# A graph layer on one core: the attention's projection in half-size products, another place for the MLP's token sums, two key loads on another queue, and an earlier start of the graph's steps

## The chip, the cores and the metric

The kernel runs on one core of a Trainium2 chip. Its time is device microseconds (us) of one execution; the number compared is the median of several executions. The engines have short names: PE is TensorE (matrix products, with PEld for its weight loads), DVE is VectorE, ACT is ScalarE, POOL is GpSimd, SP is SyncE. SP, ACT and POOL also issue transfers (DMA). Each engine works through its own queue in order, so an instruction that waits holds up all that stand behind it on that engine.

## What is computed

All data is 32-bit float. 1250 nodes with 768 features go through three blocks, whose results are added to the features:

```python
xn = layernorm(x)                                   # [1250, 768]
x1 = x + gnn(xn) + mix(xn)
out = x1 + ffn(layernorm(x1))

def gnn(xn):            # two layers of graph attention, 4 heads of 192, then 2 heads of 96
    e = leaky_relu(s_src[src] + s_dst[dst], 0.2)    # 21250 edges with the loops
    ee = exp(e - segment_max(e, dst)[dst])
    out = segment_sum(ee / segment_sum(ee, dst)[dst] * h[src], dst)
    ...

def mix(x):
    q, k, v = split(layernorm(x) @ qkv_w + qkv_b)   # 12 heads of 64
    q, k = elu(q) + 1, elu(k) + 1
    kv = einsum('sd,se->de', k, v)                  # per head
    y = (q @ kv) / (q @ k.sum(0))
    x = x + y @ proj_w + proj_b                     # the projection
    h = gelu(layernorm(x) @ fc1_w + fc1_b) @ fc2_w + fc2_b   # the MLP, 768 -> 3072 -> 768
    return x + h

def ffn(x):             # 4 experts of 768 -> 1536 -> 768; the router picks 2 for all nodes
    ...
```

## The kernel before

The tokens lie in 10 tiles of 125. Tokens 0 to 624 and 625 to 1249 are treated as two halves, since most large products are made by Strassen's scheme (Winograd's form): both operands are cut into quarters, four sums are made on each side, and seven half-size products take the place of eight. `combined` (and `seven_weights`) makes the four sums of the weights' side, `differences` (and `by_tokens`) the four of the tokens' side; one of each four overwrites a quarter in place. `product` issues a half product as three accumulating matmuls. Each 32-bit matmul instruction shows as two records in the trace.

The order of the work:

1. Weights are folded, x is normalized, x @ Wu is made (L545). Meanwhile the graph's edges are turned into a dense table of edge counts: in 10 pieces of 17 columns of 125 edges each, DVE compares the edges' keys (loaded as rows, `kr`, by `load_keys` and `later_pieces`) with the piece's own keys, and POOL writes each column by an indirect transfer that adds into one of two tables in memory (`tab`, L315; 170 in all, columns alternate between the tables). The tables are cleared by SP's transfers of `pattern`. The keys of pieces 0 to 3 are loaded by POOL's queue (L276), pieces 4 to 9 by SP's.
2. The graph's first features (L578), then keys and values, then queries of the attention (`keys_pair`, `values_pair`, `queries`). `divided` makes the attention's denominators (a small product `ps_z`, a reciprocal L943, a product L944), `project` folds kv into the projection's weights `pm`.
3. The projection: for each tile and each half of the output columns six accumulating matmuls (L974), added by DVE (L979) to the normalized features, which come back from memory (`xn_d`). After each group of tiles (`order2`) come moments (L409), a normalization (L997), transposes (L1004) and scalings by `affine` (odd blocks on ACT, even ones on DVE, L372). When the last tile is through, the tokens' side of the MLP, `xt`, gets memory that the attention's tiles have left, and `by_tokens` fills it (L105).
4. The MLP in 12 groups of 256 hidden columns, each with two units of tokens (250 and 375 of either half): `fc1_unit` yields after each of its seven half products, `fc2_half` makes two matmuls for one tile and one half of the output columns (L1077) and DVE adds them (L1082). A string, `PPhhhhPhhPPhhPPhhhh` and the like, sets how products (P) and halves (h) alternate.
5. The graph attention is a generator, `gnn()`, whose steps are spread over the MLP: after every P and h `spend` adds to a credit, and each step taken costs some. The credit starts at -44, so that the first step comes 42 us of nominal work after spending begins, and spending begins with the first group's second unit. The graph's first step merges the two tables (`merged`, L1115), fetches the rows of the sum (L1128), and DVE turns each fetched block of 125 rows into `far` (L1143), from which running maxima per head are made (L1151, L1147). The products of the attention weights follow (L1255, L1294).
6. The expert layer (L81, L1655) and the output.

The framework assigns memory by pools that open and close, adds the semaphores, and fixes each engine's order when the kernel is built; `pin` keeps an instruction in the order of the program.

Of the kernel before, what the change touches and what calls it, by code (L numbers as in the profile page):

```python
# [8 lines left out]
F32 = mybir.dt.float32  # L9
# [23 lines left out]
def tile_gps_layer(ctx, tc, a, out):  # L33
# [6 lines left out]
    def bcast(ap, p):  # L40
        return ap.partition_broadcast(p)
# [181 lines left out]
    arow = ep.tile([TP, 2, D], F32, name="arow")  # L223
    nc.sync.dma_start(arow[:, 0, :], bcast(a["L0_gnn_bu"], TP))
    nc.sync.dma_start(arow[:, 1, :], bcast(a["L0_mix_fc2_b"], TP))
    kvb = rp.tile([128, 2, D], F32, name="kvb")
    kb, vb = kvb[:TP, 0, :], kvb[:, 1, :]
    nc.sync.dma_start(kb, bcast(a["L0_mix_qkv_b"][D : 2 * D], TP))
    nc.sync.dma_start(vb, bcast(a["L0_mix_qkv_b"][2 * D : 3 * D], 128))
    ones = ep.tile([96, TP], F32, name="ones")  # L230
    nc.gpsimd.memset(ones, 1.0)

# [8 lines left out]
        )  # L241
        pin(nc.gpsimd.dma_start(key_d, key))

    kcol = rp.tile([TP, EC], F32, name="kcol")

    def columns():
        ps = bank4("ps_key")
# [10 lines left out]
    )  # L258


    counts_of = rp.tile([128, TP], BF16, name="counts_of")
# [307 lines left out]
    for t in range(NT):  # L569
# [40 lines left out]
            nc.sync.dma_start(brow_d, arow[0:1, 0, :])  # L610
        if t == 8:
            edges.close()
            mk = mix.enter_context(tc.tile_pool(name="mk", bufs=1, side="right"))

            def between(name):
                return mk.tile([128, 384], F32, name=name, bufs=2)
# [17 lines left out]
    with tc.tile_pool(name="kvp", bufs=1) as kvp:  # L634
# [13 lines left out]
        kvbd = mk.tile([128, KC, 128], F32, name="kvbd")  # L648
        ksum = mk.tile([128, KC, 128], F32, name="ksum")
# [245 lines left out]
    with tc.tile_pool(name="qp", bufs=1) as qp:  # L895
# [56 lines left out]
                if 4 <= n < 10:  # L952
                    project(n - 4)
        acc, xn = xn, acc
        divided(5, (0,))
        rest_of = [1, 2, 3]


        mv2 = const.tile([TP, NT, 2], F32, name="mv2")
        r2 = const.tile([TP, NT, 2], F32, name="r2")  # L960
        order2 = [(0, 1, 5, 6), (2, 3, 7), (4, 8), (9,)]
        for part in order2:
            for t in part:
                by_parts(nc.sync, xn[:, t, :], xn_d[t])
        at = 0
        for part in order2:
            where = {t: at + i for i, t in enumerate(part)}
            ts = slice(at, at + len(part))
            at += len(part)
            for t in part:  # L970
                for c0, w in HALVES:
                    ps = bank("ps_p")
                    for k in range(KC):
                        nc.tensor.matmul(  # L974
                            ps[:TP, :w], qT[:, k, t * TP : (t + 1) * TP], pm[:, k, c0 : c0 + w],
                            start=k == 0, stop=k == KC - 1,
                        )
                    o = xn[:, t, c0 : c0 + w]
                    nc.vector.tensor_tensor(o, ps[:TP, :w], o, ALU.add)  # L979
                    if rest_of:  # L980
                        divided(5, (rest_of.pop(0),))
# [12 lines left out]
            for t in part:  # L994
                z = qp.tile([TP, D], F32, name="z2", bufs=2)
                i = where[t]
                nc.scalar.activation(  # L997
                    z, xn[:, t, :], AF.Identity, bias=r2[:, i, 1:2], scale=r2[:, i, 0:1]
                )
                for j in range(2):  # L1000
                    ps = bank4("ps_t")
                    for i in range(3):
                        k = 3 * j + i
                        nc.tensor.transpose(  # L1004
                            ps[:, i, :TP], z[:, k * 128 : (k + 1) * 128], ident[:TP, :TP]
                        )
                    for i in range(3):
                        k = 3 * j + i
                        affine(
                            fT[:, k, t * TP : (t + 1) * TP], ps[:, i, :TP], k, "ln2_w", "ln2_b"  # L1010
                        )
# [382 lines left out]
    for g in range(GROUPS):  # L1394
        if g:
            load_fc1(g + 1)
            load_fc2(g, 1)
            load_fc2(g + 1, 0)
        for c, pattern in enumerate(("PPhhhhPhhPPhhPPhhhh", "PPhhPhhPPhhPPhh")):
            if g == GROUPS - 1 and c:  # L1400
                for _ in steps:
                    pass
                cost = None
                gnn_pool.__exit__(None, None, None)
            parts = fc1_unit(g, c)
            for p in pattern:
                if p == "P":
                    next(parts)
                    if g or c:
                        spend(2.04 if c else 1.36)  # L1410
                elif todo:
                    put_half(*todo.pop(0))
            todo = halves_of(g, c)
    for x in todo:
        put_half(*x)
    turned(ready[0])

    t9 = NT - 1
# [442 lines left out]
```

## Time and profile before

| what | value |
|---|---|
| median of 3 runs (lowest, highest) | 1904.69 us (1903.83, 1906.24) |
| the profiled execution: its time, its span | 1900.13 us, 1898.2 us |
| busy: PE, PEld, DVE, ACT, POOL | 1869.0, 1245.7, 1336.0, 803.3, 498.0 us |
| mean granted TensorE clock | 0.994 |
| the table's scatters on POOL (L315) | 57.2 to 562.3 us, 170 |
| the projection (L974) | 432.9 to 520.6 us, 240 records |
| first matmul of the MLP, last of its halves | 521.2 us, 1330 us |
| the graph's first instruction on DVE (L1143) | 590.5 us |

Times in the profile are us from the span's start. In a line of the timeline the columns are start, length, engine, source line, operation, what is written and read, shapes, number of instructions, and in brackets how long the engine had been idle and what ended that. A wait view tells "who <- for whom: us in total, times, longest". The span is 1.93 us shorter than the execution.

### The profile page before, as it was taken

To read this page: it belongs to the slowest core of one execution; us is meant where nothing else is said; L and a number is where in the kernel's file an instruction comes from. 1 tells how busy PE (TensorE), PEld (TensorE's weight loads), DVE (VectorE), ACT (ScalarE), POOL (GpSimd) and SP (SyncE) were. 2 spreads that over 40 slices of the span, in tenths; PEclk is the share of its full clock that TensorE was granted. 3 is DMA by queue.
4 is the path that set the end of the run, shared out by engine and by line. 5 is a ranking of instruction groups with operands and counts; after the bars stand their busy time and mean duration, and the time that the engine had idled before them with its cause. 6 is when DMAs were issued, how large, how long until landed. Compare 5 with 4: busy or idle time off the path is not lost.

```text
span 1898.2 us, 19544 instructions
## 1 busy us (share of the span) xinstructions
PE 1869.0 (98%) x6966; PEld 1245.7 (66%) x6966; DVE 1336.0 (70%) x2407; ACT 803.3 (42%) x1207; POOL 498.0 (26%) x341
## 2 busy tenths in 40 slices
PE   9999999999998999999999999999999999999998
PEld 7555556865565668787777655566766666666664
DVE  4656692677546967676666977766677777777778
ACT  3233221331321128777674186645364353433330
POOL 2265766687882110111111121000221000000000
PEclk9999999999998999999999999999999999999999
DMA  9748532523139751233343532202485201011023
GB/s 341 238 97 213 114 85 52 134 19 49 2 30 187 136 145 55 70 95 88 106 113 79 151 111 73 69 9 67 126 101 82 71 0 67 3 64 47 12 87 109
DMA packets 184285, 175.50 MB, mean 92 GB/s; under 512 B 110043, under 2 KB 153595, under 8 KB 182908
## 3 DMA queue, kind: packets, MB, share of 16 engines
q0 software_dynamic: 126640, 68.01, 20.8%
q1 hardware_dynamic: 54270, 98.48, 16.4%
q10 hardware_dynamic: 3278, 7.75, 1.3%
q8 instruction: 55, 0.90, 0.2%
q14 instruction: 42, 0.34, 0.1%
HBM read 137.80 MB, written 42.05 MB: 95 GB/s over the span
## 4 chain that ended last, share of the span: by engine, by line
PE 91%; DMA 4%; POOL 1%; DVE 1%; issue 1%; ACT 1%; SPq 0%; DVEq 0%; POOLq 0%; ACTq 0%
PE ps_f L1077 14%; PE ps_p L81 13%; PE ps_r L81 12%; PE ps_o L1255 7%; PE ps_a L127 7%; PE ps_g L578 4%; PE ps_u L545 4%; PE ps_p L974 4%; PE ps_c L127 3%; PE ps_f L1655 3%; PE ps_o L1294 2%; PE ps_va L127 2%; PE ps_ka L127 2%; PE ps_qa L127 2%; PE ps_d L127 2%; POOL tab L315 1%
## 5 line engine op out<-in xcount | busy, mean ns | idle before, releaser
L315 POOL DMA_INDIRECT tab<-mult,place_e x170 | 351.1, 2065 | 157.7 <-DMA tab<-mult,place_e 102.6
L1077 PE MATMUL ps_f<-w,v 128*125 128x384 f32 x960 | 338.9, 487 | 6.9 <-DVE slot_a L1082 6.9
L1077 PEld LDWEIGHTS ps_f<-w,v 128*125 128x125 f32 x960 | 178.0, 188 | 113.4 <-DVE slot_a L1082 8.0
L1082 DVE TENSOR_TENSOR slot_a<-ps_f,slot_a 125x384 f32<-125x384 f32 x240 | 131.6, 553 | 66.6 <-PE ps_f L1077 62.7
L1210 DVE TENSOR_TENSOR wt<-ee 125x375 f32<-125x375 f32 (+1 forms) x180 | 105.9, 590 | 84.5 <-PE ps_o L1255 57.5
L1255 PEld LDWEIGHTS ps_o<-turns,wt 125*125 125x125 f32 x800 | 137.1, 188 | 29.1 <-DVE wt L1211 4.0
L1255 PE MATMUL ps_o<-turns,wt 125*125 125x193 f32 x800 | 151.7, 329 | 2.9 <-DVE wt L1211 2.9
L1205 ACT ACTIVATE ee<-bt,s 125x375 f32<-125x375 f32 (+1 forms) x180 | 114.8, 638 | 77.1 <-DVE wt L1210 69.8
L81 PE MATMUL ps_p<-fT,w 128*128 128x312 f32 (+1 forms) x432 | 125.5, 426 | 0.6 <-ACT c L1573 0.6
L1211 DVE SCALAR_TENSOR_TENSOR wt<-wt,slot_x 125x375 f32<-125x375 f32 (+1 forms) x180 | 105.9, 590 | 4.4
L81 PEld LDWEIGHTS ps_p<-fT,w 128*128 128x128 f32 x432 | 81.5, 189 | 36.2 <-ACT c L1573 1.1
L81 PE MATMUL ps_r<-w,slot_a 128*125 128x384 f32 x260 | 94.5, 486 | 0.0
L127 PE MATMUL ps_a<-fT,w 128*128 128x250 f32 (+1 forms) x288 | 86.8, 432 | 0.7 <-DVE slot_a L979 0.7
L1617 DVE SCALAR_TENSOR_TENSOR slot_x<-ps_r,gate,slot_x 125x384 f32<-125x384 f32 x100 | 60.7, 615 | 33.3 <-PE ps_r L81 33.0
L81 PE MATMUL ps_p<-xt,ws 128*128 128x313 f32 (+1 forms) x288 | 83.6, 426 | 0.0
L578 PE MATMUL ps_g<-fx,zT 128*125 128x388 f32 x240 | 80.2, 490 | 1.5 <-DVE zT L372 1.5
L545 PE MATMUL ps_u<-wu,fT 128*125 128x384 f32 x240 | 79.9, 487 | 0.4 <-ACT fT L531 0.4
L974 PE MATMUL ps_p<-wp,slot_x 128*125 128x384 f32 x240 | 79.9, 486 | 0.0
L1147 DVE SCALAR_TENSOR_TENSOR slot_x<-turns,s,slot_x 125x1250 f32<-125x1250 f32 x54 | 79.4, 1512 | 0.1
L1026 ACT ACTIVATE v<-v,par 128x250 f32<-128x250 f32 (+1 forms) x72 | 40.0, 556 | 88.0 <-DVE v L1046 41.3
L1208 ACT ACTIVATE ee<-bt,s1l 125x375 f32<-125x375 f32 (+1 forms) x120 | 75.4, 628 | 0.1
L81 PE MATMUL ps_r<-w2s,ht 128*125 128x384 f32 x200 | 72.7, 486 | 0.0
(403 smaller groups left out, 3413.0 us busy)
## 6 DMA issues: line engine op xcount, KB each, us to landing
turns<-g_d POOLq DMA_DIRECT2D x12, 942.4 KB, 14.2
w<-in_L_mix_fc_w_dram SPq DMA_DIRECT2D x12, 768.0 KB
w<-in_L_mix_fc_w_dram SPq DMA_DIRECT2D x24, 384.0 KB
slot_x<-tab POOLq DMA_DIRECT2D x14, 610.4 KB, 6.6
w<-in_L_ffn_w_dram SPq DMA_DIRECT2D x11, 768.0 KB
w<-in_L_ffn_w_dram SPq DMA_DIRECT2D x5, 1536.0 KB
slot_x<-tab POOLq DMA_DIRECT2D x40, 183.1 KB, 3.3
kr_l<-key_d SPq DMA_DIRECT2D x6, 1062.5 KB
```

The costliest lines, as they stand in the source:

```text
L81: return lambda *args, **kw: pin(getattr(self.engine, name)(*args, **kw))
L127: engine.matmul(ps, wt[:, k, :], x[:, k, :], start=k == 0 and not more, stop=k == n - 1, skip_group_check=more,)
L315: nc.gpsimd.indirect_dma_start(out=tabs[c % 2][:, :], out_offset=bass.IndirectOffsetOnAxis(ap=place[:, c : c + 1], axis=0), in_=mult[:, c ...
L545: nc.tensor.matmul(ps[:TP, :w], fT[:, k, tc_], wu[:, k, c0 : c0 + w], start=k == 0, stop=k == KC - 1,)
L578: nc.tensor.matmul(ps[:TP, :388], zT[:, k, :], fx[:, k, h2 * 388 : (h2 + 1) * 388], start=k == 0, stop=k == KC - 1,)
L974: nc.tensor.matmul(ps[:TP, :w], qT[:, k, t * TP : (t + 1) * TP], pm[:, k, c0 : c0 + w], start=k == 0, stop=k == KC - 1,)
L1077: nc.tensor.matmul(ps, v_of[c][:, f, h, at : at + TP], lasts[g, j][:, f, :], start=f == 0, stop=f == 1,)
L1082: nc.vector.tensor_tensor(o, ps, o, ALU.add)
L1205: nc.scalar.activation(e[:, 0, :w], bt[:TP, 0, :w], AF.Exp, bias=s[:, 0, h, c : c + 1])
L1210: nc.vector.tensor_tensor(wt[:, :w], e[:, 0, :w], e[:, 1, :w], ALU.max)
L1211: nc.vector.scalar_tensor_tensor(wt[:, :w], wt[:, :w], 1.0, adj, op0=ALU.min, op1=ALU.mult)
L1255: nc.tensor.matmul(sums[i // 2][:TP, (i % 2) * 193 : (i % 2 + 1) * 193], wt[:, i * TP : (i + 1) * TP], gh[:, c, :], start=c == 0 and i % 2 ...
```

## The change

The diff does six things. The projection is made by seven half products for each pair of tiles t and t + 5 (`projected`), with the weights' sums in `wsum` and the tokens' differences in the memory of the query weights (`xq`); `order2` becomes four parts of 2, 2, 4 and 2 tiles. A place `room` of 9 x 625 columns is opened when the edges' first memory closes; it holds the key and value biases (loaded there and then, no longer at the start), `kvbd`, `ksum` and the attention's intermediates (`between`), and later `xt`. `by_tokens` of the MLP's first unit and the first group's weight sums move from the end of the last part to the end of the third. In all but the last part all scalings go to ACT. The keys of pieces 2 and 3 are loaded by SP. The graph's credit starts at -20 instead of -44, its pace is 1.01 instead of 1.05, and the string of the first group's second unit changes.

```diff
-    rp = mix.enter_context(tc.tile_pool(name="rp", bufs=1, side="right"))
...
-    kvb = rp.tile([128, 2, D], F32, name="kvb")
-    kb, vb = kvb[:TP, 0, :], kvb[:, 1, :]
-    nc.sync.dma_start(kb, bcast(a["L0_mix_qkv_b"][D : 2 * D], TP))
-    nc.sync.dma_start(vb, bcast(a["L0_mix_qkv_b"][2 * D : 3 * D], 128))
...
-            load_keys(i + 2, nc.gpsimd)
+            load_keys(i + 2, nc.sync)
...
-    def affine(o, v, k, wname, bname):
-        if k % 2:
+    def affine(o, v, k, wname, bname, scalar=False):
+        if k % 2 or scalar:
...
         if t == 8:
             edges.close()
+            xt_pool = ExitStack()
+            xt_room = xt_pool.enter_context(tc.tile_pool(name="xt_room", bufs=1, side="right"))
+            room = xt_room.tile([128, 9 * HALF], F32, name="room")
+            kvb = room[:, : 2 * D].rearrange("p (j d) -> p j d", d=D)
+            kb, vb = kvb[:TP, 0, :], kvb[:, 1, :]
+            nc.sync.dma_start(kb, bcast(a["L0_mix_qkv_b"][D : 2 * D], TP))
+            nc.sync.dma_start(vb, bcast(a["L0_mix_qkv_b"][2 * D : 3 * D], 128))
+            kvbd, ksum = (
+                room[:, c : c + D].rearrange("p (k n) -> p k n", n=128) for c in (2 * D, 3 * D)
+            )
+            turn = {}
+            def between(name):
+                n = turn[name] = turn.get(name, -1) + 1
+                c = 4 * D + 384 * (2 * ("c1", "u2", "ex").index(name) + n % 2)
+                return room[:, c : c + 384]
...
-        divided(5, (0,))
-        rest_of = [1, 2, 3]
+        xq = wq_of[0].rearrange("p k d -> p (k d)")[:, : 4 * 9 * TP].rearrange(
+            "p (u a b n) -> p u a b n", u=4, a=3, b=3
+        )
+        def pair_differences(t):
+            of = (
+                qT[:, k : k + 3, h * HALF + t * TP : h * HALF + (t + 1) * TP]
+                for k in (0, 3) for h in (0, 1)
+            )
+            differences(nc.vector, of, xq[:, t % 4], 0, TP)
+        def projected(t):
+            cs, ds = slice(t * TP, (t + 1) * TP), slice(HALF + t * TP, HALF + (t + 1) * TP)
+            x11, x21, x22, t3 = qT[:, 0:3, cs], qT[:, 3:6, cs], qT[:, 3:6, ds], qT[:, 0:3, ds]
+            t1, t2, t4 = (xq[:, t % 4, i] for i in range(3))
+            pa, pd, pc = (bank(n)[:TP, :384] for n in ("ps_pa", "ps_pd", "ps_pc"))
+            w11, w12 = pm[:, 0:3, 0:384], pm[:, 3:6, 0:384]
+            def put(o, ps):
+                nc.vector.tensor_tensor(o, ps, o, ALU.add)
...
+            product(nc.tensor, pa, x11, w11)
+            put(y11, pa)
+            yield
+            product(nc.tensor, pd, x21, w12)
+            put(y11, pd)
+            yield
+            _, _, s3, w22, s1, s2, s4 = sevens["p"]
+            product(nc.tensor, pa, t2, s2, more=True)
+            put(y21, pa)
+            yield
+            product(nc.tensor, pc, t1, s1)
+            put(y22, pc)
+            yield
+            product(nc.tensor, pa, t3, s3, more=True)
+            put(y22, pa)
+            yield
+            product(nc.tensor, pc, x22, s4, more=True)
+            put(y21, pc)
+            yield
+            product(nc.tensor, pa, t4, w22, more=True)
+            put(y12, pa)
+            yield
...
-        order2 = [(0, 1, 5, 6), (2, 3, 7), (4, 8), (9,)]
+        order2 = [(0, 5), (1, 6), (2, 7, 3, 8), (9, 4)]
...
+        pairs2 = [projected(t) for t in range(NT // 2)]
+        take(pairs2[0], 2)
+        take(pairs2[1], 2)
+        sevens["p"] = seven_weights(pm, wsum)
+        pair_differences(0)
+        xt = room.rearrange("p (a b n) -> p a b n", a=3, b=3)
...
+            for t in part[::2]:
+                t = t % 5
+                if t:
+                    pair_differences(t)
+                for i, _ in enumerate(pairs2[t]):
+                    if t == 0 and i < 4:
+                        divided(5, (i,))
...
-            if at == NT:
-                mix.close()
-                mix_t = mlps.enter_context(tc.tile_pool(name="mix_t", bufs=1, side="right"))
-                xt = mix_t.tile([128, 3, 3, HALF], F32, name="xt")
-                by_tokens(nc.vector, xt, *MIX[0])
-                fc1_sums(0)
...
-            if at == NT:
-                by_tokens(nc.vector, xt, *MIX[1])
+            if part[0] == 2:
+                by_tokens(nc.vector, xt, *MIX[0])
+                fc1_sums(0)
+        mix.close()
+        by_tokens(nc.vector, xt, *MIX[1])
...
-    credit, cost = -44.0, 0.0
+    credit, cost = -20.0, 0.0
...
-        credit += 1.05 * us
+        credit += 1.01 * us
...
+            if g == 0 and c:
+                pattern = "PhPhhPhhhPhhPPP"
```

More of the change, by code (lines that the diff above doesn't have):

```diff
@@ L242, in compute_keys @@
         pin(nc.gpsimd.dma_start(key_d, key))
-    kcol = rp.tile([TP, EC], F32, name="kcol")
+    kcol = lw.tile([TP, EC], F32, name="kcol")
     def columns():
@@ L258, in tile_gps_layer @@
     )
-    counts_of = rp.tile([128, TP], BF16, name="counts_of")
+    counts_of = lw.tile([128, TP], BF16, name="counts_of")
     nc.gpsimd.memset(counts_of, 256.0)
@@ L612, in tile_gps_layer @@
             edges.close()
+            xt_pool = ExitStack()
[13 more added lines that the diff above has]
+                return room[:, c : c + 384]
             mk = mix.enter_context(tc.tile_pool(name="mk", bufs=1, side="right"))
-            def between(name):
-                return mk.tile([128, 384], F32, name=name, bufs=2)
             edges = ExitStack()
@@ L647, in tile_gps_layer @@
             pin(nc.vector.memset(same[b, b], 1.0))
-        kvbd = mk.tile([128, KC, 128], F32, name="kvbd")
-        ksum = mk.tile([128, KC, 128], F32, name="ksum")
         p_kv = [bank4("ps_kv"), bank4("ps_kv")]
@@ L954, in tile_gps_layer @@
         acc, xn = xn, acc
-        divided(5, (0,))
-        rest_of = [1, 2, 3]
+        xq = wq_of[0].rearrange("p k d -> p (k d)")[:, : 4 * 9 * TP].rearrange(
[15 more added lines that the diff above has]
+                nc.vector.tensor_tensor(o, ps, o, ALU.add)
+            y11, y12, y21, y22 = (
+                xn[:, u, c0 : c0 + 384] for u in (t, t + 5) for c0 in (0, 384)
+            )
+            product(nc.tensor, pa, x11, w11)
[20 more added lines that the diff above has]
+            yield
         mv2 = const.tile([TP, NT, 2], F32, name="mv2")
         r2 = const.tile([TP, NT, 2], F32, name="r2")
-        order2 = [(0, 1, 5, 6), (2, 3, 7), (4, 8), (9,)]
+        order2 = [(0, 5), (1, 6), (2, 7, 3, 8), (9, 4)]
         for part in order2:
@@ L969, in tile_gps_layer @@
             at += len(part)
-            for t in part:
[L971 to L981, printed above, removed]
-                moments(xn[:, t, :], mv2[:, where[t], :])
-            if at == NT:
-                mix.close()
-                mix_t = mlps.enter_context(tc.tile_pool(name="mix_t", bufs=1, side="right"))
-                xt = mix_t.tile([128, 3, 3, HALF], F32, name="xt")
-                by_tokens(nc.vector, xt, *MIX[0])
-                fc1_sums(0)
+            for t in part[::2]:
[5 more added lines that the diff above has]
+                        divided(5, (i,))
+            for t in part:
+                moments(xn[:, t, :], mv2[:, where[t], :])
             r, nb = r2[:, ts, 0], r2[:, ts, 1]
@@ L1009, in tile_gps_layer @@
                         affine(
-                            fT[:, k, t * TP : (t + 1) * TP], ps[:, i, :TP], k, "ln2_w", "ln2_b"
-                        )
-            if at == NT:
-                by_tokens(nc.vector, xt, *MIX[1])
+                            fT[:, k, t * TP : (t + 1) * TP], ps[:, i, :TP], k, "ln2_w", "ln2_b",
+                            at < NT,
+                        )
+            if part[0] == 2:
[3 more added lines that the diff above has]
+        by_tokens(nc.vector, xt, *MIX[1])
     banks.close()
@@ L1415, in tile_gps_layer @@
         put_half(*x)
+    xt_pool.close()
     turned(ready[0])
```

## The prediction

> **What bounds the kernel now.** I read the page's first part, the waits of TensorE (PE), the timelines of PE, VectorE (DVE) and GpSimd (POOL) around those waits, and then followed back what the longest one waited for.
>
> ```profile
> PE 1869.0 (98%) x6966; PEld 1245.7 (66%) x6966; DVE 1336.0 (70%) x2407; ACT 803.3 (42%) x1207; POOL 498.0 (26%) x341
> ```
>
> PE is busy 1869.0 of 1898.2 us. So the end can only come earlier by matmul time taken out, or out of the 29 us in which PE stands still. PE's longest wait (view of waits, engine PE), and the same place in the timelines of PE and DVE:
>
> ```profile
> PE ps_f L1077 <- DVE slot_a L1082: 6.9, 1, 6.9
> ```
>
> ```profile
> 587.51 1.45 PE L1077 MATMUL ps_f<-w,v 128*125 128x384 f32 x4
> 595.83 2.92 PE L1077 MATMUL ps_f<-w,v 128*125 128x384 f32 x4 [6.86 <-DVE slot_a L1082]
> 598.54 3.52 PE L127 MATMUL ps_a<-fT,w 128*128 128x375 f32 x6
> ```
>
> ```profile
> 579.46 0.56 DVE L1082 TENSOR_TENSOR slot_a<-ps_f,slot_a 125x384 f32<-125x384 f32 x1 [0.73 <-PE ps_f L1077]
> 590.54 0.96 DVE L1143 TENSOR_SCALAR turns<-slot_x 125x1250 f32<-125x1250 f32 x1 [10.53 <-DMA slot_x<-tab]
> ```
>
> PE waits for an eviction (L1082) that has nothing wrong with it: it is queued on DVE behind L1143, the graph's first instruction, which stands still 10.5 us for the first rows of the edge table. After the wait PE is also slow for two groups: four matmuls take 2.92 us instead of 1.45, six take 3.52 instead of 2.05, so 2.9 us more. Where the table is late shows in POOL's timeline:
>
> ```profile
> 52.27 0.53 POOL L276 DMA_DIRECT2D kr<-key_d  x1 [30.65 <-DVE eq L295]
> 57.18 2.12 POOL L315 DMA_INDIRECT tab<-mult,place_e  x1 [4.38 <-DVE place_e L313]
> 71.38 2.00 POOL L315 DMA_INDIRECT tab<-mult,place_e  x1 [12.08 <-DMA tab<-mult,place_e]
> 83.09 1.98 POOL L315 DMA_INDIRECT tab<-mult,place_e  x1 [9.71 <-DMA tab<-mult,place_e]
> 89.62 3.76 POOL L315 DMA_INDIRECT tab<-mult,place_e  x1 [4.55 <-DMA tab<-mult,place_e]
> ...
> 99.28 1.98 POOL L315 DMA_INDIRECT tab<-mult,place_e  x1 [1.90 <-DMA tab<-mult,place_e]
> 100.49 1.40 POOL L276 DMA_DIRECT2D kr<-key_d  x1
> 102.19 2.02 POOL L315 DMA_INDIRECT tab<-mult,place_e  x1 [0.30 <-issue]
> ...
> 560.30 2.00 POOL L315 DMA_INDIRECT tab<-mult,place_e  x1 [0.30 <-issue]
> 564.44 4.63 POOL L1115 DMA_DIRECT2D tab<-tab  x3 [2.14 <-DMA tab<-mult,place_e]
> 576.00 0.57 POOL L1128 DMA_DIRECT2D slot_x<-tab  x1 [6.93 <-PE ps_f L1077]
> ```
>
> 170 scatters run from 57.18 to 560.30, late ones every 2.3 us, and from the last of them the merges and the first fetch take 30.2 us to 590.54. No matmul sets this chain: POOL and its transfers do. Call the end of it R, the moment at which the table is readable: 590.5.
>
> **The change, part by part.** *The graph's first step.* In the built order the changed kernel has L1143 behind 9 of the 240 evictions L1082; before it stood behind 20. DVE then waits for R much earlier in PE's work, and all later L1082, L1046 and L1059 wait behind it. PE's order gives the price. With the trace's spacing (1.27 us for a product of 250 columns, 1.90 for 375, 1.29 for a half of fc2, 0.65 for a tile's transposes) PE stood before at 67.0 us of work after the MLP's first matmul: 7 products of the first unit, 7 of the second, 7 of the third, 3 of the fourth, 23 halves (521.2 + 67.0 = 588.2; the trace says 588.9). In the new order it runs out of its three PSUM buffers at half 13, at 42.7 us. So 24.3 us of work that lay ahead of the wait comes behind it. Against this, DVE now has just L1143 (0.96) and one eviction (0.47) to do until PE goes on, 1.5 us after R instead of 5.3: minus 3.8. With R unchanged the end moves by +20.5 us, and every us by which R comes earlier takes one off. When the MLP begins does not matter to this, as long as PE gets to its block, about 43 us in, before R: it has until about 540.
>
> *R: the keys on SyncE.* Two loads of 1062.5 KB leave POOL's queue. The first (52.27) lay directly ahead of the first scatter; its landing took 10.9 us, to 63.2, and the scatter landed by 71.1. The first six scatters go to one table and each waits for the one before, so this delay is passed on: I take 6 us off. The second (100.49) cost POOL 1.40 us of issue, 0.30 of gap and about 2.8 in the scatters at 107 to 111: 4 us off. Against this SyncE now issues both keys at about 73.5, behind L225 (73.13), in place of the two key and value bias loads (384 + 375 KB) that move to 179: 1.37 MB more while scatters two to four run, at the 154 to 222 GB/s of 70 to 82 us some 7 us of traffic, of which I charge 2 to the scatters, and 1 more at 179. Behind the new SyncE waits stand only the router's loads and L568 at 116.33, which nobody needs sooner; the third keys land by about 87 (73.5 + the 13.1 of the slowest key load) and are read at 89.20. From 308 us on scatters are at 2.3 us each and gain nothing. So scatters end 7 to 8 us earlier; another 1 for the first fetch, which no longer meets SyncE's loads of 566 to 580. Bounds: worse by 3, if the keys on the other queue slow the serial scatters as much as they did in their own; better by 38, if the first 17 scatters, 76.85 us from 57.18 to 134.03, ran at 2.3 each (39 us). Value taken: 9. It lies near the low end because of the 102.6 us that POOL waits for scatters (view of waits, engine POOL) the rows put only 6 + 2.8 down to the two loads; the other bursts (the 5.6 MB clear of the second table, bias rows, wk, stores) stay.
>
> The Trainium skill ("DMA: Bandwidth & Descriptors", section "Issuing engines are not separate DMA queues") says that transfers of all issuing engines end on the same 16 DMA engines and that another issuer saves only its own issue time. By that rule the gain would be the 1.9 us of POOL's issue and the sum +18.6 rather than +11.5. The same page (section "Queues, rings and completion order") has engines take turns between queues, which speaks for more; the scatter's 13.9 us behind the keys' 10.9 is the row for it here.
>
> *Seven half products.* 240 L974 matmuls become 210; 72 of them in a row take 23.38 us, 0.3225 each with the overlap: minus 9.7 us of PE. DVE gets 35 evictions instead of 20 (15 x 0.55 = 8.3), four sums (4 x 1.36 = 5.4) and 20 differences (20 x 0.54 = 10.8), and gives 24 scalings (L372, 0.41) to ScalarE: +14.7 net on 63.9 busy of the 98 us from 432 to 530. ScalarE gets 24 x 0.455 = 10.9 on 27.4 busy. The sum is not the point; the place is:
>
> ```profile
> 438.61 4.86 DVE L943 RECIPROCAL rz<-ps_z 128x375 f32<-128x375 f32 x2
> 444.24 0.55 DVE L979 TENSOR_TENSOR slot_a<-ps_p,slot_a 125x384 f32<-125x384 f32 x1
> ```
>
> DVE is late when this stage begins: its first eviction runs at 444.24, though PE had that product by 434.95. Before, six PSUM buffers hid that. Now the products need sums and differences that stand in the same queue. From 417.6 to the second pair's first difference DVE's new order has 10 reciprocals (2.42), 37 small operations (0.45) and four sums (1.27), 46 us, so it comes at about 464. PE needs it after nine products (1.94) and six sums over heads (0.65) from 432.2, so at 453.5. PE waits 10 us or so, up to 14 with the shorter waits on the way. That takes back the 9.7: the MLP begins between 519 and 526, before it was 521.2. Both are before 540, so this part gives nothing to the end here; if R were no bound, the part would be worth between -9.7 and +4.
>
> *The rest.* The place xt gets (room) lets the first tokens' side be made in the third part; behind the last product PE has 16.6 us of the first MLP unit and of halves to cover the last tiles, as it had before: 0, up to 3 if the two tiles at the end instead of one come late. Biases at 179 are first read at 201.7 (L680): covered; uncovered, 0.76 MB at 154 GB/s, 5 us. Pace 1.01: last graph weights stand behind 208 evictions, before 209, so the tail is unchanged; PE's waits between 600 and 1345 are 4.1 us in all, so pace is worth -4 to +4; taken 0.
>
> Sum: +24.3 - 3.8 - 9 = +11.5 us. The profiled execution took 1900.13 us, so its like would take 1911.6; the median of the three runs is 1904.69, 4.6 above, so the forecast is **1916 us**.
>
> **Rivals.** *The table comes in time (faster).* If R falls by over 24.3 us the sum changes sign clearly, and past about 30 PE no longer waits: the 6.9 wait and the 2.9 of slow matmuls go, and the projection's -9.7 to +4 counts: 1885 to 1899, say 1894. For it: piece 0 alone loses 38 us to waits. Against: the first two waits (12.1 and 9.7) fall where the DMA share by stretches is 1.00 (58 to 64), 1.06 (64 to 70) and 0.90 (70 to 76), and SyncE's own traffic, which stays, makes most of that. 0.13. *Break-even.* R earlier by 17 to 24 us: within 0.2% of no change, 1904. 0.11. *R does not come earlier.* The keys on SyncE load the same engines beside the scatters: R -0 to +3, the time 1925 to 1929, or above with a late projection. 0.06 for above the forecast's own range of +4 to +24, which has 0.70.
>
> **How the numbers follow.** A measurement here can tell 0.2%, 3.8 us, from no change. Faster 0.13, same 0.11, slower 0.70 + 0.06 = 0.76. The range reaches from 1902, which leaves out little more than the fast rival, to 1929, R later by 3: 0.8 inside.
>
> **What would show it.** DVE's first L1143 with an idle time of 20 us or more (10.5 before) and PE waiting for L1082 at half 13, over 15 us, then two slow groups; last scatter at about 552; PE waiting for DVE some 10 us between 441 and 466; MLP's first matmul at 519 to 526. It is wrong if the last scatter starts before 540, or if PE has no wait over 10 us after 530.

## The result, and the profile after

| | before | changed |
|---|---|---|
| median, 10 runs each on one chip | 1902.74 us (1899.19 to 1907.02) | 1919.49 us (1910.37 to 1927.57) |
| ratio of the times, 95% interval | | 1.0085 (1.0066 to 1.0103) |
| the profiled execution: time, span | 1900.13, 1898.2 | 1916.69, 1914.9 |

The changed kernel is 16.8 us slower. "R" is, as in the prediction, the moment at which the table is readable: the start of DVE's first L1143, which is L1200 in the changed kernel. Other lines move likewise: L315 is now L310, L1077 is L1134, L1082 is L1139, L1255 is L1312; L979's place is taken by L985.

The page's first line for PE, and the first answers of the view of waits, engine PE:

```profile
PE 1857.6 (97%) x6936; PEld 1235.9 (65%) x6936; DVE 1352.0 (71%) x2422; ACT 814.0 (43%) x1233; POOL 495.4 (26%) x339
```

```profile
PE ps_f L1134 <- DVE slot_a L1139: 25.0, 1, 25.0
PE ps_pc L127 <- DVE wq L105: 7.0, 1, 7.0
```

PE has 11.4 us less matmul time and the kernel is longer all the same: its standing time went from 29 to 57 us. One wait carries most of it, 25.0 where before's was 6.9. The same place in the timelines of PE, then DVE:

```profile
563.22 5.32 PE L1134 MATMUL ps_f<-w,v 128*125 128x384 f32 x16
568.38 1.43 PE L127 MATMUL ps_a<-room,ws 128*128 128x250 f32 x6
594.78 4.38 PE L1134 MATMUL ps_f<-w,v 128*125 128x384 f32 x8 [24.97 <-DVE slot_a L1139]
```

```profile
564.71 0.56 DVE L1139 TENSOR_TENSOR slot_a<-ps_f,slot_a 125x384 f32<-125x384 f32 x1 [0.80 <-PE ps_f L1134]
593.23 1.03 DVE L1200 TENSOR_SCALAR turns<-slot_x 125x1250 f32<-125x1250 f32 x1 [27.96 <-DMA slot_x<-tab]
594.18 0.54 DVE L1139 TENSOR_TENSOR slot_a<-ps_f,slot_a 125x384 f32<-125x384 f32 x1
```

DVE does one eviction at 564.71 and then stands 28 us in front of L1200 for the table. The evictions that PE needs are queued behind it. PE goes on 1.55 us after R. How the table came to be no earlier, in POOL's timeline:

```profile
57.10 2.13 POOL L310 DMA_INDIRECT tab<-mult,place_e  x1 [35.23 <-DVE place_e L308]
70.69 2.01 POOL L310 DMA_INDIRECT tab<-mult,place_e  x1 [11.47 <-DMA tab<-mult,place_e]
85.82 1.99 POOL L310 DMA_INDIRECT tab<-mult,place_e  x1 [13.12 <-DMA tab<-mult,place_e]
91.90 2.72 POOL L310 DMA_INDIRECT tab<-mult,place_e  x1 [4.09 <-DMA tab<-mult,place_e]
...
183.00 1.99 POOL L310 DMA_INDIRECT tab<-mult,place_e  x1 [2.91 <-DMA tab<-mult,place_e]
193.84 1.99 POOL L310 DMA_INDIRECT tab<-mult,place_e  x1 [8.85 <-DMA tab<-mult,place_e]
...
563.99 1.99 POOL L310 DMA_INDIRECT tab<-mult,place_e  x1 [1.79 <-DMA tab<-mult,place_e]
568.28 4.59 POOL L1172 DMA_DIRECT2D tab<-tab  x3 [2.30 <-DMA tab<-mult,place_e]
579.02 0.58 POOL L1185 DMA_DIRECT2D slot_x<-tab  x1 [6.15 <-issue]
```

No key load stands on POOL any more between the scatters, and the first two waits are still 11.5 and 13.1 us (before 12.1 and 9.7). The 33rd scatter starts at 183.00, against 190.06 before: 7 us earlier. The 34th waits 8.85 us for the one before it, and from there this execution runs level with before's. The last one starts at 563.99, not earlier than before's 560.30, and R is 593.23, not 590.54.

The projection's stage, PE and then DVE:

```profile
444.62 2.17 PE L127 MATMUL ps_pc<-wsum,wq 128*125 128x384 f32 x6 [1.74 <-DVE wsum L114]
465.21 1.64 PE L127 MATMUL ps_pc<-wsum,wq 128*125 128x384 f32 x2 [6.96 <-DVE wq L105]
```

```profile
459.43 2.49 DVE L950 RECIPROCAL rz<-ps_z 128x375 f32<-128x375 f32 x1
461.85 0.48 DVE L985 TENSOR_TENSOR slot_a<-ps_pa,slot_a 125x384 f32<-125x384 f32 x1
464.63 0.52 DVE L105 TENSOR_TENSOR wq<-slot_x 128x375 f32<-128x375 f32 x1
```

PE stands 10.4 us in five waits between 441 and 466, most of it for the second pair's differences (L105, from 464.63), which are queued behind reciprocals. The MLP's first matmul comes at 524.45 (before 521.23).

### The profile page after: what moved, and what is told of

It is laid out like the page before. It is cut to its first block, busy times and chain, and to the rows that moved or that the text cites. A ratio compares the mean times of both kernels' runs of the same rounds, so it can differ in the third digit from the quotient of the medians.

```text
span 1914.9 us, 19540 instructions
## 1 busy us (share of the span) xinstructions
PE 1857.6 (97%) x6936; PEld 1235.9 (65%) x6936; DVE 1352.0 (71%) x2422; ACT 814.0 (43%) x1233; POOL 495.4 (26%) x339
## 3 DMA queue, kind: packets, MB, share of 16 engines
q0 software_dynamic: 126352, 65.84, 20.5%
q1 hardware_dynamic: 54558, 100.66, 16.8%
## 4 chain that ended last, share of the span: by engine, by line
PE 89%; DVE 3%; DMA 3%; issue 2%; POOL 1%; ACT 1%; ACTq 0%; DVEq 0%; POOLq 0%
PE ps_f L1134 15%; PE ps_p L81 13%; PE ps_r L81 12%; PE ps_a L127 7%; PE ps_o L1312 7%; PE ps_u L540 4%; PE ps_c L127 3%; PE ps_g L573 3%; PE ps_f L1715 3%; PE ps_o L1351 2%; PE ps_va L127 2%; PE ps_ka L127 2%; PE ps_qa L127 2%; PE ps_d L127 2%; PE ps_u L1364 1%
## 5 line engine op out<-in xcount | busy, mean ns | idle before, releaser
L310 POOL DMA_INDIRECT tab<-mult,place_e x170 | 349.5, 2056 | 194.6 <-DMA tab<-mult,place_e 113.0
L1134 PE MATMUL ps_f<-w,v 128*125 128x384 f32 x960 | 339.0, 487 | 25.0 <-DVE slot_a L1139 25.0
L1134 PEld LDWEIGHTS ps_f<-w,v 128*125 128x125 f32 x960 | 178.0, 188 | 131.2 <-DVE slot_a L1139 26.0
L1139 DVE TENSOR_TENSOR slot_a<-ps_f,slot_a 125x384 f32<-125x384 f32 x240 | 131.9, 553 | 61.7 <-PE ps_f L1134 57.6
L1312 PEld LDWEIGHTS ps_o<-turns,wt 125*125 125x125 f32 x800 | 136.0, 187 | 26.0 <-issue 0.8
L1312 PE MATMUL ps_o<-turns,wt 125*125 125x193 f32 x800 | 149.6, 327 | 0.0
L573 PE MATMUL ps_g<-fx,zT 128*125 128x388 f32 x240 | 80.2, 490 | 1.5 <-DVE zT L367 1.5
L127 PEld LDWEIGHTS ps_a<-fT,w 128*128 128x128 f32 x288 | 53.7, 189 | 24.6 <-issue 1.5
```

Source lines behind the costliest of these rows:

```text
L127: engine.matmul(ps, wt[:, k, :], x[:, k, :], start=k == 0 and not more, stop=k == n - 1, skip_group_check=more,)
L310: nc.gpsimd.indirect_dma_start(out=tabs[c % 2][:, :], out_offset=bass.IndirectOffsetOnAxis(ap=place[:, c : c + 1], axis=0), in_=mult[:, c ...
L573: nc.tensor.matmul(ps[:TP, :388], zT[:, k, :], fx[:, k, h2 * 388 : (h2 + 1) * 388], start=k == 0, stop=k == KC - 1,)
L1134: nc.tensor.matmul(ps, v_of[c][:, f, h, at : at + TP], lasts[g, j][:, f, :], start=f == 0, stop=f == 1,)
L1139: nc.vector.tensor_tensor(o, ps, o, ALU.add)
L1312: nc.tensor.matmul(sums[i // 2][:TP, (i % 2) * 193 : (i % 2 + 1) * 193], wt[:, i * TP : (i + 1) * TP], gh[:, c, :], start=c == 0 and i % 2 ...
```

## The experiments

Each kernel was timed beside the kernel before on its own chip. Chips differ: before's median was 1902.7, 1894.9, 1898.0, 1899.5 and 1900.5 on five, and before's own runs spread over some 17 us. So ratios are compared, or kernels on the same chip. The kernels of the first four runs shared a chip, so did the next four, and the three after them.

**Is it the start of the graph?** The first run takes the start back and leaves the rest of the change; the second is the start alone. The start here is credit, pace and string together; they were not separated. Some lines of the diffs here and below are shortened.

```diff
  e1, on the changed kernel           e2, on the kernel before
-    credit = -20.0                  -    credit = -44.0
+    credit = -44.0                  +    credit = -20.0
-    credit += 1.01 * us             -    credit += 1.05 * us
+    credit += 1.05 * us             +    credit += 1.01 * us
-    pattern = "PhPhhPhhhPhhPPP"     +    pattern = "PhPhhPhhhPhhPPP"   (first group's second unit)
```

> The changed kernel with the graph's start set back (credit -44, pace 1.05, the old string); projection, room and keys stay as changed. Theory (the moment R at which the edge table is readable, 593.2 in the changed kernel, sets the time, and only how much of PE's work lies behind the wait for it matters): PE stops again at half 23, about 67.8 us after the MLP's first matmul (524.5 + 67.8 = 592.3), goes on at R + 5.3 = 598.5, so one wait of about 6 us where the changed kernel has 25; against before's 595.83 that is +2.7, time about 1905 (1902 to 1908), MLP's first matmul at 524 as in the changed kernel. Rival (the projection by half products and the room cost the time themselves): time stays at 1915 to 1920.

> The kernel before with the graph's start alone (credit -20, pace 1.01, the changed string). Theory: R stays at 590.5, PE stops at half 13, some 24 us of work earlier, and goes on at R + 1.5 = 592: a wait of 22 to 28 us, first matmul of the MLP at 521.2 as before, time +16 to +21 on before, 1919 to 1924. Rival (the projection and the room cost the time): a time within 4 us of before, 1899 to 1907. Rival (the pace or the string of the products costs it): the wait is under 15 us and the loss lies behind 600.

With the start undone: 1901.39 against 1894.93 of before, 1.0029 (1.0009 to 1.0050). The expected wait of 6 us isn't there: PE began the MLP at 526.2 and has one more tile's transposes and 1.6 us of waits inside it, so that it needed the eviction at about 596, and with R at 591.23 the eviction came at 595.8. Its longest waits in the view of waits are those of the projection and of the graph's first product:

```profile
PE ps_pc L127 <- DVE wq L105: 7.0, 1, 7.0
PE ps_o L1312 <- DVE wt L1268: 3.5, 1, 3.5
```

With the start alone: 1912.86, 1.0082 (1.0049 to 1.0114), the whole loss of the change on a kernel that has nothing else of it. Timeline of DVE, then PE:

```profile
596.29 0.81 DVE L1143 TENSOR_SCALAR turns<-slot_x 125x1250 f32<-125x1250 f32 x1 [35.61 <-DMA slot_x<-tab]
```

```profile
597.62 5.48 PE L1077 MATMUL ps_f<-w,v 128*125 128x384 f32 x8 [32.40 <-DVE slot_a L1082]
```

So the start is the cause: alone it brings the whole loss, and without it 0.29% of the 0.85% is left. The wait is over the expected 22 to 28 because R came at 596.3 in this execution, 6 us later than in the profile before, though no scatter ahead of it differs.

**What did the moved loads do to R?** Five kernels: the keys alone on the kernel before; the keys back on GpSimd's queue; the changed kernel itself again; the biases early again; and both loads back.

```diff
  e3, on the kernel before:       -  load_keys(i + 2, nc.gpsimd)
                                  +  load_keys(i + 2, nc.sync)
  e4 and e7, on the changed one:  -  load_keys(i + 2, nc.sync)
                                  +  load_keys(i + 2, nc.gpsimd)
  e6 and e7, on the changed one:  -  kvb = room[:, : 2 * D]              (loaded when the place opens, at 179)
                                  +  kvb = lw.tile([128, 2, D], F32)     (loaded behind arow, as before)
```

> The kernel before with the keys of pieces 2 and 3 on SyncE and nothing else; the bias loads stay in their early place. Theory (the keys on SyncE gain 5 to 9 us, and in the changed kernel the bias loads at 179 gave it back at scatter 34): the last scatter starts at 552 to 556 against 560.3, R at 581 to 586, PE's wait of 6.9 shrinks to under 2 and the time falls by 5 to 9: 1893 to 1898. Rival (the keys on SyncE do nothing that lasts, the gain up to 183 us came from the biases that no longer load at 73): last scatter 558 to 563, R 588 to 594, time 1899 to 1906.

> The changed kernel with the keys of pieces 2 and 3 on GpSimd's queue again; biases at 179 stay. Theory (keys on SyncE gain, biases at 179 take): the scatters from 20 to 33 lie 5 to 9 us later than in the changed kernel, the last one at 566 to 573, R at 596 to 602, PE's wait 28 to 33, time 1922 to 1928. Rival (what the scatters gained up to 183 came from the biases leaving 73 us): scatters as in the changed kernel within 3 us, R 591 to 596, time 1916 to 1922.

> The changed kernel as it is, beside the next two on the same chip, as their measure: in these three PE always waits for R, so their times differ by just what their R differ. R + 1324 is the time of the profiled runs so far (593.2 and 1916.7). Theory: a wait for L1139 of 15 to 30 us in the profile, time R + 1322 to R + 1327. Rival (something else than R sets the time): the sum is off by more than 4.

> The changed kernel with the key and value biases in a place of their own, loaded in their early place at 71 to 75 us again, keys still on SyncE. Theory (the bias loads at 179 gave the keys' gain back): R 5 to 9 us earlier than in the changed kernel on the same chip, time lower by 5 to 9. Rival (the scatters' start differs by several us from execution to execution, and neither loads moved by the change matter to R): time within 3 us of the changed kernel.

> The changed kernel with both moves of loads undone: keys of pieces 2 and 3 on GpSimd's queue, biases early. Prediction's step (the two moves bring R forward by 9): time 9 us higher than the changed kernel on the same chip. Theory (they do nothing that lasts; the drift of R by itself is as large): within 3 us of it.

First, R does set the time. In every kernel with the early start PE waits at this place, and the profiled execution's time follows its R (e9 is told of further on):

| kernel | R | time | time - R |
|---|---|---|---|
| both loads back (e7) | 584.04 | 1908.39 | 1324.4 |
| keys back (e4) | 587.05 | 1912.76 | 1325.7 |
| reordered (e9) | 590.07 | 1913.46 | 1323.4 |
| changed again (e5) | 592.14 | 1915.59 | 1323.5 |
| changed | 593.23 | 1916.69 | 1323.5 |
| biases early (e6) | 593.70 | 1919.63 | 1325.9 |
| start alone (e2) | 596.29 | 1922.05 | 1325.8 |

R moves over 12 us here and the remainder stays within 2.5. The two ends, DVE and PE of the kernel with both loads back:

```profile
584.04 0.88 DVE L1201 TENSOR_SCALAR turns<-slot_x 125x1250 f32<-125x1250 f32 x1 [16.95 <-DMA slot_x<-tab]
```

```profile
585.44 4.90 PE L1135 MATMUL ps_f<-w,v 128*125 128x384 f32 x8 [13.80 <-DVE slot_a L1140]
```

Second, the loads hardly move R. On one chip the changed kernel has a median of 1916.06 (6 runs), with the biases early 1919.70 (6 runs), with both back 1919.44 (7 runs). The means of the changed one and of both back, 1915.8 and 1918.6, differ by 2.8, with some 5 either way from the runs' own spread. That is neither clearly more than nothing nor the 9 of the prediction. With the biases early the mean is 5.1 above the changed kernel's, with 4.5 either way. The keys alone gave 1903.03, 1.0030 (1.0009 to 1.0052): no gain at all; the keys back 1915.46, 1.0111 (1.0077 to 1.0145).

Third, R drifts by itself. The scatters in each profiled execution, us from POOL's timeline; the 18th scatter is the first of the second piece:

| keys, biases | last scatter starts at | from the first to the third | from the first to the 18th |
|---|---|---|---|
| GpSimd, early (before, e2, e7, e8) | 560.30, 568.81, 556.17, 563.28 | 25.9, 26.1, 25.7, 25.6 | 80.2, 78.0, 74.9, 78.3 |
| SyncE, at 179 (changed, e1, e5, e9 to e12) | 563.99, 563.43, 565.54, 562.27, 563.89, 568.07, 560.93 | 27.8 to 28.7 | 72.9 to 75.3 |
| SyncE, early (e3, e6) | 558.95, 566.49 | 28.8, 27.8 | 78.0, 77.8 |
| GpSimd, at 179 (e4) | 558.33 | 25.4 | 72.5 |

In the last scatter the first row spreads over 12.6 us with the same loads; the means of the first two rows are 562.1 and 564.0. In the pair for which it was followed the drift is late: in the kernel before and in the one with the start alone the 61st scatter starts at 276.0 and 276.5, the last ones lie 8.5 us apart. The theory that the biases at 179 took the gain back falls: with the biases early and the keys on SyncE the third piece of scatters begins at 194.0 (e6), with the biases at 179 at 188.1 to 196.9. What of the 7 us at the 33rd scatter is lost at the 34th or 35th isn't the biases' work; what it is stays open.

The two last columns show what each move does early on. With the keys on SyncE the third scatter comes some 2.5 us later in every execution. The first piece is shorter where the biases load at 179, by some 3 us in the mean (74.5 against 77.9; only e7's 74.9 overlaps), and with the biases early it is no shorter for the keys on SyncE. So the early gain in the changed kernel goes with the biases, which no longer load in the first piece, and not with the keys' queue.

Why the keys alone were slower than nothing isn't settled either. In its one profile PE had no wait at R (588.56), but began some 3 us late; the graph's weights landed late, long before any key load, which gives 2.2 of it:

```profile
9.86 1.88 PE L385 MATMUL ps_wT<-ident,fT 128*96 128x128 f32 x8 [2.19 <-DMA fT<-in_L_gnn_W_dram]
```

**If the early start costs, does a later one gain?**

```diff
  e8, on the kernel before
-    credit, cost = -44.0, 0.0
+    credit, cost = -71.0, 0.0
-        credit += 1.05 * us
+        credit += 1.08 * us
```

> The kernel before with nothing but a later start of the graph (credit -71 in place of -44, pace 1.08 in place of 1.05, so that the steps still end before the last group's second unit). Theory (PE waits only where R comes after its work runs out): PE runs out some 22 us later, which covers an R of up to 605; no wait for L1082, time at the lowest that the kernel before reaches (1888.5 of 23 runs on one chip), 1887 to 1892, and the spread of its runs falls from 17 us to under 6. Rival (denser steps make the graph or the tail late): 1895 or more, with new waits behind 1200.

1895.12 (1892.62 to 1897.61) against 1897.96 (1888.71 to 1903.65) of before: 0.9989 (0.9971 to 1.0006). As expected no wait is left at R, and the spread is 5 us instead of 15; the expected 1887 to 1892 was not reached. DVE comes to L1143 at 601.58, after the table:

```profile
601.58 0.80 DVE L1143 TENSOR_SCALAR turns<-slot_x 125x1250 f32<-125x1250 f32 x1
```

But the lowest run is 4 us above before's lowest. The MLP from its first matmul to its last halves takes 802.6 us, against 799.5 in the kernel with the keys alone, which did not wait for R either. Of these 3.1 us some 0.6 are longer waits for the graph's products (3.7 and 2.0 us, there 3.5 and 1.6) and 0.9 is a wait for weight sums (L114); the rest is open. So a later start gives evenness, and no time that is clear of the noise.

**What is the projection worth when R doesn't bound?** Three kernels with the projection's order on DVE as the question: the reorder with the early start, then a late start without and with it.

```diff
  reorder (e9, e11), on the changed kernel
+        pair_differences(1)            (behind pair_differences(0), ahead of the first pair's products)
-                if t:
+                if t > 1:
                     pair_differences(t)
-                    if t == 0 and i < 4:
+                    if t == 1 and i < 4:
                         divided(5, (i,))
  late start (e10, e11): credit -71, pace 1.08, the string of the changed kernel taken out
```

> The changed kernel, start as changed, with two steps of the projection reordered: the second pair's differences stand ahead of the first pair's last five products, and the four last denominators (reciprocals of 2.5 us on DVE) among the second pair's products. Theory (R alone sets the time of the changed kernel): the wait of 7.0 for L105 and the slow matmuls behind it go, the MLP's first matmul comes at 515 to 518 instead of 524.5, PE's wait for L1139 grows by as much, to 28 to 35, and the time stays within 3 of the changed kernel, 1914 to 1921, R + 1324. Rival (the lateness of the projection counts): time 7 to 9 lower, 1906 to 1912.

> The changed kernel with a late start of the graph (credit -71, pace 1.08, the old string). Theory (with the late start R no longer bounds, and then the half products in this place cost about 7 to 10 against the full ones, as the lowest runs of the kernel with the start undone, 1899.4, against the lowest of before, 1888.5, say): no wait for L1139, 1898 to 1905, 4 to 9 above the kernel before with the same late start (1895.1). Rival (the half products gain their 9.7 us of matmul once R doesn't bound): 1883 to 1889.

> The same with the projection reordered as in the run of that name: late start, old string. Theory (the half products' gain was lost in DVE's order, 10.4 us of waits and slow matmuls behind them): 7 to 10 below the kernel without the reorder, 1889 to 1896, and 5 to 10 below the kernel before on the same chip, spread of runs under 6. Rival (DVE has too much work in the stage, so that the waits only move to later parts): within 3 of the kernel without the reorder, the MLP's first matmul at 521 to 525.

The reorder missed its aim. With the early start the MLP's first matmul came at 526.9, not at 515 to 518, so that run doesn't separate the theories; its time, 1913.73 (1.0074, 1.0050 to 1.0098), is again R + 1323.4. With the late start: 1901.24 (1.0006, 0.9990 to 1.0022) without the reorder, 1900.48 (1.0004, 0.9987 to 1.0021) with it. So the waits only moved, as the rival said. PE of the late start with the reorder:

```profile
446.70 1.61 PE L127 MATMUL ps_pc<-wsum,wq 128*125 128x384 f32 x2 [2.93 <-DVE wsum L114]
478.15 0.91 PE L127 MATMUL ps_pd<-wp,slot_x 128*125 128x384 f32 x2 [1.30 <-DVE slot_x L951]
482.88 1.64 PE L127 MATMUL ps_pc<-wsum,wq 128*125 128x384 f32 x2 [3.82 <-DVE wq L105]
```

The four reciprocals now stood in front of the third pair's differences instead of the second's. The last run leaves them where they were and moves only the second pair's differences, behind the second reciprocal; its start lies between before's and the late one.

```diff
  e12, on the changed kernel
-                if t:
+                if t > 1:
                     pair_differences(t)
                 for i, _ in enumerate(pairs2[t]):
                     if t == 0 and i < 4:
                         divided(5, (i,))
+                    if t == 0 and i == 1:
+                        pair_differences(1)
-    credit = -20.0, pace 1.01, pattern "PhPhhPhhhPhhPPP"
+    credit = -58.0, pace 1.05, the old string
```

> The changed kernel with the denominators left among the first pair's products, only the second pair's differences moved ahead (behind the second denominator), the old string, and the graph's start between before's and the late one (credit -58, pace 1.05). In the built order the second pair's products then need nothing that stands behind the denominators. Theory (what the half products lost is one wait in DVE's order, 7.0 and 1.9 of slow matmuls behind it): no wait for L105 over 3 us between 441 and 490, MLP's first matmul at 516 to 520 against 524.5, no wait for L1139 or under 3, time 1891 to 1896, faster than the kernel before on the same chip by 0.2 to 0.6%. Rival (DVE's work in the stage is too much, the wait moves as in the first reorder): MLP's first matmul at 522 to 527, time 1898 to 1902.

1891.31 (1890.07 to 1893.79) against 1900.48: 0.9956 (0.9938 to 0.9974), faster than both kernels. PE and DVE:

```profile
446.64 2.17 PE L127 MATMUL ps_pc<-wsum,wq 128*125 128x384 f32 x6 [1.67 <-DVE wsum L114]
469.08 2.20 PE L127 MATMUL ps_pa<-wp,slot_x 128*125 128x384 f32 x6 [1.06 <-DVE slot_a L985]
518.63 1.53 PE L127 MATMUL ps_a<-fT,w 128*128 128x250 f32 x6 [0.65 <-DVE slot_a L985]
```

```profile
591.91 0.83 DVE L1202 TENSOR_SCALAR turns<-slot_x 125x1250 f32<-125x1250 f32 x1 [1.28 <-DMA slot_x<-tab]
```

The wait of 7.0 is gone. The MLP begins 9.0 us earlier than in the kernel with the first reorder (518.63 against 527.59, both executions 2 us late from their start), and its length is 0.9 less, 802.1 against 803.0. So nearly all that separates these two comes from the order on DVE in the projection, not from the start between them. From the projection's first matmul to the MLP's first it is 88.4 us before, 91.4 in the changed kernel, 92.4 with the late start and the first reorder, and 83.5 in this one: 4.9 less than before. How much of its 0.44% comes from its start is open: that start was not run by itself, and the still later one alone gave 0.9989. DVE comes to the table 1.3 us before it is readable, and PE doesn't wait for it.

## Why the prediction was right, step by step

The forecast was slower, 1916 within 1902 to 1929; it is 1919.5, and the mechanism is the one it named. Its marks: DVE idle by 20 or more ahead of the first L1143 (28.0); PE waiting at half 13 for over 15 (25.0); PE late by some 10 us between 441 and 466 (10.4); the MLP at 519 to 526 (524.45). All these came. Of the two slow groups behind the wait one came. And "last scatter at about 552" did not: it was 563.99. That the time lies so near the forecast is partly luck: in the profiles R came 11.7 us later than forecast, and the early start cost 6.6 less at a given R.

*The graph's first step, +24.3 and -3.8.* PE went on 1.55 us after R, as said. At a given R the change cost less than the 20.5 of these two terms: time - R was 1309.6 before and is 1323.5, so +13.9. Two differences that the profiles show make 5.7 of the missing 6.6. The matmuls behind the wait lose 1.6 us (eight take 4.38; the unhindered eight take 2.74), not 2.9. And the early start takes away a wait that the sum did not have: before, the graph's first product waited 2.91 us and then ran at half rate (2.94 for eight); in the changed kernel it runs at once, sixteen in 2.80. PE before, then changed:

```profile
714.25 2.94 PE L1255 MATMUL ps_o<-turns,wt 125*125 125x193 f32 x8 [2.91 <-DVE wt L1211]
```

```profile
716.23 2.80 PE L1312 MATMUL ps_o<-turns,wt 125*125 125x193 f32 x16
```

*R, the keys on SyncE, -9.* This is the term that was mis-sized. The profile after has +2.7, the kernels on one chip put the two moved loads at -2.8 with some 5 either way; the bounds of the step (-38 to +3) hold both. Its reason failed early and late. The first scatter was to land 6 us earlier without the key load ahead of it; the second one, which waits for that, starts at 70.69 instead of 71.38. The third now starts later, at 85.82 instead of 83.09: the DMA share by stretches is 1.03 from 76 to 82 us, before it was 0.62. The prediction charged 2 us for that traffic, about what all executions show. The second piece does begin at 132.2 instead of 137.3, but this goes with the biases, as the table above shows; with the keys back on GpSimd it begins at 129.55. And by the third piece, at 196.1 against 195.7, nothing was left. The prediction also read the scatters from 308 us on as 2.3 us each; in the profile before they take 2.5 from there to the last one, with 18.7 us of waits among them. The rival "R does not come earlier" was the nearer account of R, while the smaller cost of the wait made up for most of its effect on the time.

The Trainium skill ("DMA: Bandwidth & Descriptors", section "Issuing engines are not separate DMA queues") has another issuer save only its own issue time. The 2.8 measured on one chip, for both moves together, agrees with the prediction's estimate of 1.9 by that rule as well as with nothing, and speaks against the 9; the sum by it, +18.6, stood nearer to the 16.8 measured than the forecast's +11.5.

*Seven half products, nothing while R bounds.* Confirmed for the time by the start alone, which costs as much as the whole. The wait of 10 us and its place were right if the shorter waits are counted; for the second pair alone it was 7.0. For the other case the bracket was -9.7 to +4. With the start undone the ratio of 1.0029 puts the kernel 5.5 us (1.7 to 9.5) above before, at the bracket's upper end or over it; the stage itself is 3.0 longer in the changed profile, and one more tile's transposes now stand inside the MLP. About half of the half products' gain, 4.9 of 9.7 us, was had in another order on DVE.

*The rest.* Biases at 179, pace and place: no wait in the changed profile belongs to them.

That before's runs spread over some 17 us while the last kernel's stay within 4 fits the same reading: before, PE waits in some executions and not in others, as R falls.

## What to carry to other kernels

When an in-order engine holds the first instruction of a long side chain, ask when that chain can be ready at the latest, and put the instruction behind that: an earlier place gains nothing, and everything queued behind it waits too. A saving early in a chain of transfers isn't a saving at its end until a second point further down shows it. Products that need prepared operands are worth their matmul time only if the preparing engine has them ahead of the slow work in its queue; here the place of four small subtractions decided over some 8 us, most of the 9.7 that the scheme takes from PE: with them late the stage was 3.0 us longer than before, with them early 4.9 shorter.

## What the runs showed of the hardware

The same 170 scatters with the same loads gave a last scatter between 556.2 and 568.8 us in four executions. Such a chain of small indirect transfers beside large ones had no fixed length here, and with a standard deviation of 5.3 us among these four a single profile can't price a change to it below some 5 us.

PE's clock fell after short standstills. After 1.67 us the granted clock stayed at 1.00; after 2.93 us it was 0.55 in the next stretch, and two matmuls took 1.61 us instead of 0.81. Columns: stretch, length, then busy time and count of PE, PEld, DVE, ACT and POOL, the granted clock, the DMA share, GB/s. First the last kernel, with the wait of 1.67, then the first reorder with the late start:

```profile
446.00:449.00 3.00, 2.36 (x8) 1.44 (x9) 3.00 (x4) 0.00 (x0) 2.47 (x2) 1.00 0.14 1
```

```profile
446.00:449.00 3.00, 2.27 (x3) 0.99 (x4) 3.00 (x4) 0.00 (x0) 2.39 (x3) 0.55 0.16 6
```

Length alone does not decide. In the expert layer, at some 1390 us, PE stands 1.86 us both in the changed kernel and in the one with the keys back. In the first the granted clock stays at 1.00 and six matmuls take 1.85 us; in the second the next 3 us have 0.60, and the same six take 2.73.

The Trainium skill ("TensorE: Matmul & The Clock Gate", section "Part 1: The HAM clock gate (the "warmup" mystery)") puts the fall at one idle window of about 3.4 us, with a window that runs freely. In kind the rows agree; in length they don't: standstills of 2.93 and, once, of 1.86 us were enough here, so waits of under 3.4 us are not free.
